# A window-attention and Fourier-mixing kernel on one core: the first ten cycles of its row pipeline get an order of their own

## The chip, the cores and the metric

The kernel runs on one core of one Trainium2 chip. A core has a matrix engine (TensorE, PE in the profile), a vector engine (VectorE, DVE), a scalar engine (ScalarE, ACT), a general engine (GpSimd, POOL) and SyncE (SP), from which nearly all transfers are issued here. Each runs its own list of instructions in program order and waits for others by semaphores. The metric is the time of the kernel on the device in microseconds (us), lower is better. All data is fp32.

## The reference, cut to what matters

The input is 32 images of 56 by 56 tokens with 128 channels. Two layers follow one another:

```python
# layer 0: shifted-window attention (7x7 windows, 4 heads), on the group-normalised image
x = x + window_attention(group_norm(x))
# layer 1: Fourier mixing along both axes (DCT, 32 modes, mix of channels, inverse DCT)
# and then a feed-forward 128 -> 512 -> 128
x = x + feed_forward(fourier(group_norm(x)))
```

The attention of one window of 49 tokens is

```python
q, k, v = win @ w_qkv.T                      # 4 heads of 32 channels
attn = softmax(q @ k.T / sqrt(32) + rel_bias + shift_mask)
out = (attn @ v) @ w_proj.T + b_proj
```

Layer 1 of an image can only begin when the statistics of the whole result of layer 0 of that image are known.

## The kernel before

An image is worked on in 8 rows of 8 windows each. The unit of the program is a *cycle*: in cycle c the attention of row c is begun, and rows c-1, c-2 and c-3 are taken further. Layer 1 of an image starts ten cycles after its first row (`CONV_BEGIN = NWR + 2 = 10`), and from then on its large matmuls lie between those of the attention. In cycles 0 to 9 there is no layer-1 work at all, and the attention of image 0 (and, from cycle 8 on, of image 1) is alone.

The order on PE, ACT, DVE and POOL is the order of the program text (`manual_schedule`). The parts that the change reorders, with the line numbers by which the profile names them:

```python
def attn_qk(im, i):
    q, src = q_sb, im.xw[i][:, :RT]
    pq = attn_bank()
    nc.tensor.matmul(pq[:, :RT], lhsT=im.w[:, 0:C], rhs=src, start=True, stop=True)       # L323 PE
    nc.scalar.activation(q[:, :RT], pq[:, :RT], AF.Identity,
                         bias=im.bias[:, 0:1], scale=QS)                                  # L324 ACT
    pk = attn_bank()
    nc.tensor.matmul(pk[:, :RT], lhsT=im.w[:, C : 2 * C], rhs=src, start=True, stop=True) # L328 PE
    pk3 = pk[:, :RT].rearrange("p (w j) -> p w j", j=WT)
    nc.scalar.activation(k_sb[:, 0], pk3, AF.Identity,
                         bias=im.bias[:, 3:4], scale=heads[:, 0:1])                       # L330 ACT
    nc.vector.tensor_scalar(k_sb[:, 1], pk3, heads[:, 1:2], im.bias[:, 4:5],
                            ALU.mult, ALU.add)                                            # L333 DVE

# attn_v:         16 matmuls (L345), copy of v by ACT (L352)
# attn_scores:    32 matmuls into two banks (L367), bias and mask added by DVE, two tiles (L375)
# attn_max:       row maximum by DVE (L385), subtraction by POOL (L386)
# attn_exp:       exp by ACT (L392)
# attn_divide:    sum and reciprocal by DVE (L397, L399), product by POOL (L400)
# attn_transpose: two times 4 transposes on PE (L411), copied by DVE (L421) and ACT (L419)
# attn_values:    64 matmuls into two banks (L436), copied to oT by ACT (L469) and DVE (L467, three pieces)
# attn_project:   6 or 8 matmuls (L478), added to the image by DVE (L486), row written to memory (L492)
# attn_sums:      square by ACT (L501), two sums for the next statistics by DVE (L503)
# image_group:    4 transposes on PE (L259), copy by ACT (L269), statistics by DVE (L270), addition by POOL (L274)
# image_norm:     statistics of the next image, a chain of small operations between yields:
#                 DVE (L281) / PE (L284), DVE (L286, L288, L290) / PE (L295), DVE, POOL (L299), DVE (L301)
#                 / ACT (L306), PE (L309), DVE (L313 to L315)
```

All of these take their PSUM banks from one set of four, in turn, so each bank has to be emptied before the fourth one after it can be written:

```python
def attn_bank():
    return bank("pa", 4)
```

In cycles 0 to 9 the loop ran these steps, in this order (the calls for layer 1 do nothing there):

```python
# full_first
attn_transpose(c-2); attn_qk(c); next(norm); attn_sums(c-3); attn_divide(c-1)
# half_columns, quarters, eighths
attn_v(c); attn_scores(c); attn_values(c-2)
attn_max(c)
# full_last
next(norm); image groups of the next image; attn_exp(c); attn_project(c-2); next(norm)
```

The load of the second image is called for in cycle 2. Its groups are in cycle 4 (0, 1), cycle 5 (2, 3, 4) and cycle 6 (5, 6, 7), and its normalisation is stepped through in cycle 7.

Of the kernel before, what the change touches and what calls it, by code (L numbers as in the profile page):

```python
# [12 lines left out]
ALU = mybir.AluOpType  # L13
# [35 lines left out]
def swin_fourier_kernel(  # L49
# [266 lines left out]
        yield  # L316


    def attn_qk(im, i):

        q, src = q_sb, im.xw[i][:, :RT]
        pq = attn_bank()
        nc.tensor.matmul(pq[:, :RT], lhsT=im.w[:, 0:C], rhs=src, start=True, stop=True)  # L323
        nc.scalar.activation(  # L324
            q[:, :RT], pq[:, :RT], AF.Identity, bias=im.bias[:, 0:1], scale=QS
        )
        pk = attn_bank()
        nc.tensor.matmul(pk[:, :RT], lhsT=im.w[:, C : 2 * C], rhs=src, start=True, stop=True)  # L328
        pk3 = pk[:, :RT].rearrange("p (w j) -> p w j", j=WT)
        nc.scalar.activation(  # L330
            k_sb[:, 0], pk3, AF.Identity, bias=im.bias[:, 3:4], scale=heads[:, 0:1]
        )
        nc.vector.tensor_scalar(  # L333
            k_sb[:, 1], pk3, heads[:, 1:2], im.bias[:, 4:5], ALU.mult, ALU.add
        )

    def attn_v(im, i, r):

# [43 lines left out]
    def attn_max(r):  # L382
        a3 = a_sb[r % 3].rearrange("p t w j -> p (t w) j")[:, :, 0:WT]
        mx = small.tile([P, 2 * NWR], F32, tag="mx", name="mx")
        nc.vector.tensor_reduce(mx, a3, axis=AX.X, op=ALU.max)  # L385
        nc.gpsimd.tensor_tensor(  # L386
            a3, a3, mx.unsqueeze(2).to_broadcast([P, 2 * NWR, WT]), ALU.subtract
        )
# [82 lines left out]
    def attn_project(im, i):  # L471

        oT = im.oT
        n0, n1 = WS * i // 2, WS * (i + 1) // 2
        base = i // 2 * WS
        pp = attn_bank()
        for n in range(n0, n1):
            nc.tensor.matmul(  # L478
                pp[:TC, (n - n0) * C : (n - n0 + 1) * C],
                lhsT=oT[:, (n - base) * TC : (n - base + 1) * TC],  # L480
                rhs=wproj,
                start=True,
                stop=True,
            )
        piece = im.x[:, n0:n1]
        nc.vector.tensor_tensor(  # L486
            piece,
            pp[:TC, : (n1 - n0) * C].rearrange("p (n c) -> p n c", c=C),
            piece,
            ALU.add,  # L490
        )
        nc.sync.dma_start(  # L492
            im.scr[2 * n0 : 2 * n1].rearrange("(n r) w c -> (r w) n c", r=2), piece
        )
# [204 lines left out]
    def ff_out(im, g):  # L699
        t0, n = sum(FF_GROUPS[:g]), FF_GROUPS[g]  # L700
        k, last = n // P, n % P
        res = im.res
        out_tok = out[im.b].rearrange("h w c -> (h w) c")
        chunks = [P] * k + ([last] if last else [])
        pf = conv_bank()
        for c, m in enumerate(chunks):
            for f in range(NF):
                nc.tensor.matmul(  # L708
                    pf[:m, c * C : (c + 1) * C],
                    lhsT=im.hid[f][:, c * P : c * P + m],  # L710
                    rhs=wff2[:, f],
                    start=(f == 0),
                    stop=(f == NF - 1),
                )
        for c0, c1, m in ((0, k, P), (k, k + 1, last)):
            if m:
                nc.vector.tensor_tensor(  # L717
                    res[:m, c0:c1],
                    pf[:m, c0 * C : c1 * C].rearrange("p (n c) -> p n c", c=C),
                    res[:m, c0:c1],  # L720
                    ALU.add,
                )

        c = 0
        while c < len(chunks):
            m = chunks[c]
            o = t0 + c * P + SS * S
            if o < NT < o + m:
                nc.sync.dma_start(out_tok[o:NT], res[: NT - o, c])
                nc.sync.dma_start(out_tok[: o + m - NT], res[NT - o : m, c])  # L730
                c += 1
                continue
            e = c + 1
            while e < len(chunks) and chunks[e] == m and (o >= NT or o + (e + 1 - c) * m <= NT):
                e += 1
            o %= NT
            nc.sync.dma_start(
                out_tok[o : o + (e - c) * m].rearrange("(n p) c -> p n c", p=m), res[:m, c:e]
            )
            c = e  # L740
# [9 lines left out]
    def row(r):  # L750
        return (images[r // NWR], r % NWR) if 0 <= r < NB * NWR else (None, 0)
# [12 lines left out]
    def full_first(cycle, norm):  # L764
        im, i = row(cycle - 2)
        if im:
            attn_transpose(im, i, cycle - 2)
        im, i = row(cycle)
        if im:
            attn_qk(im, i)  # L770
        for im, c in fourier(cycle):
            for width, g in back_groups(c):
                load_modes(im, width, g)
        next(norm)
        im, i = row(cycle - 3)
        if im:
            attn_sums(im, i)
        for im, c in fourier(cycle):
            if c == 0:
                im.stats = fourier_stats(im)  # L780
                im.cols = {}
                next(im.stats)
                load_columns(im, 0)
                load_columns(im, 1)
        for im, c in fourier(cycle):
            if c in FF_AT:
                ff_in(im, FF_AT.index(c))
        for im, c in fourier(cycle):
            if c == 0:
                next(im.stats)  # L790
        if row(cycle - 1)[0]:
            attn_divide(cycle - 1)

    def half_columns(cycle):
        im, i = row(cycle)
        if im:
            attn_v(im, i, cycle)
        for im, c in fourier(cycle):
            if c == 0:
                for g in range(4):  # L800
                    transform(im, True, g)
            elif c in (1, 2):
                for g in (2 * c - 2, 2 * c - 1):
                    transform(im, False, g)
                    if c == 1:
                        load_columns(im, g + 2)
            elif c == 3:
                for g in range(4):
                    mix(im, False, g)
            elif c in (4, 5):  # L810
                for g in (2 * c - 8, 2 * c - 7):
                    mix(im, True, g)

    def quarters(cycle):
        im, i = row(cycle)
        if im:
            attn_scores(im, i, cycle)
        for im, c in fourier(cycle):
            for width, g in back_groups(c):
                modes_back(im, width, g)  # L820

    def eighths(cycle):
        im, i = row(cycle - 2)
        if im:
            attn_values(im, i, cycle - 2)

    def full_last(cycle, norm):
        next(norm)
        for im, c in fourier(cycle):
            if c in FF_AT:  # L830
                ff_out(im, FF_AT.index(c))
        b, i = divmod(cycle, NWR)
        if b + 1 < NB:
            if i == 2:
                images[b + 1] = image_begin(b + 1)
            for j in {4: (0, 1), 5: (2, 3, 4), 6: (5, 6, 7)}.get(i, ()):
                image_group(images[b + 1], j)
        if row(cycle)[0]:
            attn_exp(cycle)
        im, j = row(cycle - 2)  # L840
        if im:
            attn_project(im, j)
        next(norm)

    def nothing():
# [4 lines left out]
    with tc.manual_schedule(engines={ET.PE, ET.Activation, ET.DVE, ET.Pool}):  # L850
        images[0] = image_begin(0)
        for i in range(NWR):
            image_group(images[0], i)
        for _ in image_norm(images[0]):
            pass
        norm = nothing()
        for cycle in range(NB * NWR + CONV_BEGIN + FF_AT[-1] - NWR + 1):
            full_first(cycle, norm)
            if cycle >= CONV_BEGIN and (cycle - CONV_BEGIN) % NWR != 3:
                quarters(cycle)  # L860
                if row(cycle)[0]:
                    attn_max(cycle)
                half_columns(cycle)
                eighths(cycle)
            else:
                half_columns(cycle)
                quarters(cycle)
                eighths(cycle)
                if row(cycle)[0]:
                    attn_max(cycle)  # L870
            full_last(cycle, norm)
            b, i = divmod(cycle, NWR)
            norm = nothing()
            if i == NWR - 2 and b + 1 < NB:
                norm = image_norm(images[b + 1])
                next(norm)
# [62 lines left out]
```

## Time and profile before

| | before |
|---|---|
| time, median of 3 | 3755.23 us (3753.02 to 3755.56) |
| span of the profiled execution | 3748.9 us |
| PE busy | 3658.2 us, 98% |
| DVE / ACT / POOL busy | 2197.3 / 2131.1 / 1370.9 us |
| mean granted clock of TensorE | 0.993 |

The cycles, by the starts of their query matmuls (L323) in the timeline of PE:

| cycle | 0 | 1 | 2 | 3 | 4 | 5 | 6 | 7 | 8 | 9 | 10 |
|---|---|---|---|---|---|---|---|---|---|---|---|
| start, us | 20.07 | 29.39 | 40.39 | 48.95 | 59.97 | 68.45 | 78.08 | 87.63 | 102.03 | 112.05 | 122.02 |
| length, us | 9.32 | 11.00 | 8.56 | 11.02 | 8.48 | 9.63 | 9.55 | 14.40 | 10.02 | 9.97 | 18.52 |

How to read it: a busy share of 98% for PE says that it nearly always had something in its pipeline, not that it ran at its peak. The granted clock is the share of full speed that the throttle of TensorE allowed. A line of a group or a timeline gives the line of the program, the engine, the operation and its tiles; an idle time in brackets stands before the instruction, with what ended it. The releaser of a wait is inferred from semaphores, and where a wait was for several, the last one is named.

### The profile page before, as it was taken

Reading aid. Unit: us, or ns where it says so; the run is one execution under the profiler, and the core shown is the slowest. Engines: PE = TensorE matmul, PEld = TensorE weight load, DVE = VectorE, ACT = ScalarE, POOL = GpSimd, SP = SyncE. Lnnn points to the kernel's source line nnn. Section 1 sums busy time; section 2 is a strip of 40 time slices with the busy share of each in tenths; the row PEclk is TensorE's granted clock in tenths of the full one; section 3 lists DMA queues with packets and bytes.
Section 4 is the critical chain, followed back from the end, with each engine's and each line's share of the span. In section 5 each row is a group of like instructions: output and inputs, shape, how many; then the busy total and the mean of one; then the engine's idle time right before and its main releaser. Section 6 shows DMA issues by size and latency. Waiting matters only on the chain.

```text
span 3748.9 us, 140497 instructions
## 1 busy us (share of the span) xinstructions
PE 3658.2 (98%) x61632; PEld 2985.1 (80%) x61632; DVE 2197.3 (59%) x4619; ACT 2131.1 (57%) x3809; POOL 1370.9 (37%) x1421
## 2 busy tenths in 40 slices
PE   6799999999999999999999999999999999999998
PEld 5678888888888788888878888888887888888776
DVE  6665665556655556655556655666556566655641
ACT  3455556555565556555555565555655555655553
POOL 4333343333434333343334333333343333333321
PEclk8899999999999999999999999999999999999999
DMA  4233334334333434343343343343333333433332
GB/s 111 78 100 106 107 91 116 105 103 114 91 111 105 110 99 112 96 110 106 104 111 100 98 115 104 100 114 94 110 105 107 103 112 92 115 106 104 94 104 89
DMA packets 687779, 388.95 MB, mean 104 GB/s; under 512 B 40479, under 2 KB 658112, under 8 KB 686912
## 3 DMA queue, kind: packets, MB, share of 16 engines
q1 hardware_dynamic: 686557, 379.65, 36.7%
q8 instruction: 485, 7.95, 0.9%
q14 instruction: 126, 1.03, 0.1%
q10 hardware_dynamic: 611, 0.32, 0.0%
HBM read 218.29 MB, written 161.48 MB: 101 GB/s over the span
## 4 chain that ended last, share of the span: by engine, by line
PE 88%; DVE 7%; ACT 2%; DMA 1%; issue 1%; POOL 0%; SPq 0%; ACTq 0%; POOLq 0%; DVEq 0%
PE pc L708 20%; PE pc L688 15%; PE pa L345 7%; PE pc L572 6%; PE pc L606 5%; PE pa L367 5%; PE pa L411 5%; PE pa L478 5%; PE pc L645 5%; PE pa L436 4%; PE pa L323 4%; PE pa L328 4%; PE pa L259 2%; DVE part L503 1%; DVE st L270 1%; DVE a L375 1%
## 5 line engine op out<-in xcount | busy, mean ns | idle before, releaser
L400 POOL TENSOR_TENSOR a<-a,rs 128x784 f32<-128x784 f32 x256 | 389.5, 1521 | 1366.7 <-DVE rs L399 1254.4
L708 PE MATMUL pc<-wff,hid 128*128 128x128 f32 (+1 forms) x6400 | 778.2, 279 | 0.9 <-ACT hid L696 0.7
L708 PEld LDWEIGHTS pc<-wff,hid 128*128 128x128 f32 (+1 forms) x6400 | 731.0, 189 | 21.0 <-issue 1.9
L688 PE MATMUL pc<-xf,wff 128*128 128x512 f32 (+2 forms) x1792 | 712.8, 540 | 0.0
L696 ACT ACTIVATE hid<-pc,b1sb 128x512 f32<-128x512 f32 (+2 forms) x896 | 540.9, 634 | 102.0 <-PE pc L688 98.7
L688 PEld LDWEIGHTS pc<-xf,wff 128*128 128x128 f32 x1792 | 337.1, 190 | 300.4 <-issue 229.5
L386 POOL TENSOR_TENSOR a<-a,mx 128x784 f32<-128x784 f32 x256 | 389.0, 1520 | 389.2 <-DVE mx L385 384.7
L717 DVE TENSOR_TENSOR res<-pc,res 128x512 f32<-128x512 f32 (+2 forms) x256 | 143.5, 571 | 597.1 <-issue 269.8
L333 DVE TENSOR_SCALAR k<-pa,heads,bqkv 128x392 f32<-128x392 f32 x256 | 175.4, 685 | 420.0 <-ACT k L330 419.9
L419 ACT COPY aT<-pa 113x452 f32<-113x452 f32 x256 | 137.3, 536 | 475.4 <-PE pa L411 475.3
L274 POOL TENSOR_TENSOR xl<-xl,bproj 112x384 f32<-112x384 f32 (+1 forms) x256 | 291.4, 1139 | 227.3 <-PE pa L259 224.2
L392 ACT ACTIVATE a<-a 128x784 f32<-128x784 f32 x256 | 222.6, 869 | 203.5 <-POOL a L386 202.3
L375 DVE TENSOR_TENSOR a<-pa,bm 128x392 f32<-128x392 f32 x512 | 259.5, 549 | 132.1 <-PE pa L367 132.1
L352 ACT COPY v<-pa 128x512 f32<-128x512 f32 x256 | 152.4, 595 | 295.6 <-PE pa L345 295.6
L467 DVE TENSOR_SCALAR oT<-pa,bqkv 128x98 f32<-128x98 f32 (+2 forms) x768 | 171.1, 279 | 248.0 <-PE pa L436 248.0
L678 POOL TENSOR_TENSOR res<-res,b2sb 128x512 f32<-128x512 f32 (+2 forms) x256 | 263.8, 1036 | 101.0 <-DMA res<-scr 101.0
L367 PEld LDWEIGHTS pa<-k,q 64*64 64x64 f32 x8192 | 184.0, 133 | 142.7 <-issue 52.9
L345 PE MATMUL pa<-wn,xw 128*64 128x128 f32 x4096 | 282.1, 280 | 1.1 <-ACT aT L419 1.1
L345 PEld LDWEIGHTS pa<-wn,xw 128*64 128x64 f32 x4096 | 220.0, 137 | 55.3 <-issue 21.9
L478 PE MATMUL pa<-wproj,oT 128*112 128x128 f32 x1792 | 239.3, 274 | 14.3 <-DVE oT L467 11.3
L411 PE MATMUL pa<-ident,a 113*113 113x113 f32 x2048 | 250.0, 265 | 1.5 <-POOL a L400 1.5
L367 PE MATMUL pa<-k,q 64*64 64x98 f32 x8192 | 233.4, 250 | 18.5 <-DVE k L333 18.5
(87 smaller groups left out, 5939.7 us busy)
## 6 DMA issues: line engine op xcount, KB each, us to landing
zscr<-z SPq DMA_DIRECT2D x512, 112.0 KB
htok<-scr SPq DMA_DIRECT2D x256, 196.0 KB
zT<-zscr SPq DMA_DIRECT2D x192, 256.0 KB
res<-scr SPq DMA_DIRECT2D x160, 256.0 KB
out_dram<-res SPq DMA_DIRECT2D x128, 256.0 KB
scr<-xl SPq DMA_DIRECT2D x128, 224.0 KB
xl<-in_x_dram SPq DMA_DIRECT2D x32, 784.0 KB
xl<-in_x_dram SPq DMA_DIRECT2D x32, 672.0 KB
```

The costliest lines, as they stand in the source:

```text
L274: nc.gpsimd.tensor_tensor(piece, piece, bproj.unsqueeze(1).to_broadcast([TC, n1 - n0, C]), ALU.add)
L345: nc.tensor.matmul(pv[hs, j * C : (j + 1) * C], lhsT=im.xw[i][:, w * WT : w * WT + JP], rhs=im.w[:, 2 * C : 3 * C], start=True, stop=True,)
L367: nc.tensor.matmul(ps[hp][HALVES[e], pr * 2 * WT : (pr + 1) * 2 * WT], lhsT=q[cs, w * WT : w * WT + JP], rhs=k_sb[cs, :, w], start=True, s ...
L375: nc.vector.tensor_tensor(a[:, 2 * hp : 2 * hp + 2, :, 0:WT].rearrange("p u w j -> p w u j"), ps[hp][:, :RT].rearrange("p (w u j) -> p w u ...
L386: nc.gpsimd.tensor_tensor(a3, a3, mx.unsqueeze(2).to_broadcast([P, 2 * NWR, WT]), ALU.subtract)
L400: nc.gpsimd.tensor_tensor(a3, a3, rs.unsqueeze(2).to_broadcast([P, 2 * NWR, WT]), ALU.mult)
L411: nc.tensor.transpose(pt[:PW, h * P : h * P + PW], a[:PW, h, 2 * hf : 2 * hf + 2].rearrange("p w j -> p (w j)")[:, :PW], ident[:PW, :PW],)
L478: nc.tensor.matmul(pp[:TC, (n - n0) * C : (n - n0 + 1) * C], lhsT=oT[:, (n - base) * TC : (n - base + 1) * TC], rhs=wproj, start=True, sto ...
L678: nc.gpsimd.tensor_tensor(res[:m, c0:c1], res[:m, c0:c1], b2sb[:m].unsqueeze(1).to_broadcast([m, c1 - c0, C]), ALU.add,)
L688: nc.tensor.matmul(ph[:, :n], lhsT=wff1[:, f * P : (f + 1) * P], rhs=xff[:, t0 : t0 + n], start=True, stop=True,)
L696: nc.scalar.activation(hf[:, :n], ph[:, :n], AF.Relu, bias=b1sb[:, f : f + 1])
L708: nc.tensor.matmul(pf[:m, c * C : (c + 1) * C], lhsT=im.hid[f][:, c * P : c * P + m], rhs=wff2[:, f], start=(f == 0), stop=(f == NF - 1),)
```

## The change

In cycles 0 to 9 the steps are put in an order of their own (`first_rows`). On PE, matmuls that need another engine's answer are to have a group that needs nothing between them and those they depend on: after q and k come the projection of row c-3 and the transposes of row c-2, then the scores; the values of row c-2 come after the scores, and v last. For that the projection moves from the end of cycle c-1 into cycle c, and the exp of row c-1 from the end of its own cycle to behind the keys of row c. In these cycles, too, the second key tile is made by ACT instead of DVE. From cycle 10 on the program is as before. The part that starts the next image is put into a function of its own.

```diff
-    def attn_qk(im, i):
+    def attn_qk(im, i, first):
...
-        nc.vector.tensor_scalar(
-            k_sb[:, 1], pk3, heads[:, 1:2], im.bias[:, 4:5], ALU.mult, ALU.add
-        )
+        if first:
+            nc.scalar.activation(
+                k_sb[:, 1], pk3, AF.Identity, bias=im.bias[:, 4:5], scale=heads[:, 1:2]
+            )
+        else:
+            nc.vector.tensor_scalar(
+                k_sb[:, 1], pk3, heads[:, 1:2], im.bias[:, 4:5], ALU.mult, ALU.add
+            )
...
+    def first_rows(cycle, norm):
+        im, i = row(cycle)
+        if im:
+            attn_qk(im, i, True)
+        if cycle:
+            attn_exp(cycle - 1)
+        next(norm)
+        last, j = row(cycle - 3)
+        if last:
+            attn_project(last, j)
+        im2, i2 = row(cycle - 2)
+        if im2:
+            attn_transpose(im2, i2, cycle - 2)
+        if cycle:
+            attn_divide(cycle - 1)
+        if im:
+            attn_scores(im, i, cycle)
+            attn_max(cycle)
+        if im2:
+            attn_values(im2, i2, cycle - 2)
+        if last:
+            attn_sums(last, j)
+        if im:
+            attn_v(im, i, cycle)
+        next(norm)
+        next_image(cycle)
+        if cycle == CONV_BEGIN - 1:
             attn_exp(cycle)
+            attn_project(im2, i2)
         next(norm)
...
         for cycle in range(NB * NWR + CONV_BEGIN + FF_AT[-1] - NWR + 1):
+            if cycle < CONV_BEGIN:
+                first_rows(cycle, norm)
             else:
+                full_first(cycle, norm)
...
```

## The prediction

> **What bounds the kernel now.** I read the page first, for the shares of the engines and the slices.
>
> ```profile
> PE 3658.2 (98%) x61632; PEld 2985.1 (80%) x61632; DVE 2197.3 (59%) x4619; ACT 2131.1 (57%) x3809; POOL 1370.9 (37%) x1421
> ...
> PE   6799999999999999999999999999999999999998
> ```
>
> TensorE (PE) bounds the whole: nine tenths or more in 37 of 40 slices, and 88% of the chain that ended last. Only the first two slices, some 190 us, have holes; the page's row of granted clock is at 8 tenths there too, and at 9 or more behind. The diff replaces the code of cycles 0 to 9, which is exactly that part, so nothing after about 122 us is touched. Next I put the cycle borders (each cycle's first query matmul, L323, from the timeline of PE) into busy time by stretch. The columns are stretch, length, then busy time (and count) of PE, PEld, DVE, ACT and POOL, granted clock, DMA share, GB/s.
>
> ```profile
> 59.97:68.45 8.48, 6.81 (x141) 5.25 (x139) 6.17 (x14) 4.16 (x9) 2.07 (x2) 0.99 0.21 60
> 87.63:102.03 14.40, 9.22 (x144) 7.20 (x143) 9.29 (x26) 5.16 (x9) 7.88 (x10) 0.85 0.11 31
> 112.05:122.02 9.97, 7.44 (x134) 5.25 (x133) 6.05 (x14) 3.79 (x7) 3.12 (x3) 0.84 0.06 17
> 122.02:140.54 18.52, 13.76 (x248) 11.56 (x247) 8.17 (x20) 7.60 (x13) 4.11 (x5) 0.74 0.33 80
> ```
>
> No engine is full in these cycles, so it is a chain of waits. Cycle 9 shows it, first on PE (start, length, what; in brackets the idle time and its releaser), then on VectorE (DVE).
>
> ```profile
> 112.05 1.54 PE L323 MATMUL pa<-xw,wn 128*128 128x392 f32 x2
> 113.39 1.50 PE L328 MATMUL pa<-xw,wn 128*128 128x392 f32 x2
> 114.81 1.09 PE L345 MATMUL pa<-wn,xw 128*64 128x128 f32 x16
> 116.44 0.90 PE L367 MATMUL pa<-k,q 64*64 64x98 f32 x32 [0.53 <-DVE k L333]
> 117.27 0.81 PE L436 MATMUL pa<-aT,v 49*32 49x49 f32 x64
> 120.08 1.10 PE L478 MATMUL pa<-wproj,oT 128*112 128x128 f32 x8 [2.00 <-DVE oT L467]
> 121.01 1.21 PE L411 MATMUL pa<-ident,a 113*113 113x113 f32 x8
> ```
> ```profile
> 115.69 0.69 DVE L333 TENSOR_SCALAR k<-pa,heads,bqkv 128x392 f32<-128x392 f32 x1 [3.48 <-ACT k L330]
> 116.30 0.54 DVE L503 TENSOR_REDUCE part<-xl 112x32 f32<-112x384 f32 x1
> ...
> 118.38 0.97 DVE L375 TENSOR_TENSOR a<-pa,bm 128x392 f32<-128x392 f32 x2
> 119.27 0.66 DVE L467 TENSOR_SCALAR oT<-pa,bqkv 128x98 f32<-128x98 f32 x3
> ```
>
> Two holes: the scores wait for the second key tile, and the projection waits about 2 us for oT. DVE idles 3.48 us until the keys come and then has everything at once: key tile, sums, softmax sum, scores, oT. And q and k took 1.54 and 1.50 us here, against 0.84 and 0.82 us at 48.95 and 49.62: each hole is followed by some microseconds at half clock.
>
> **What the Trainium skill says.** TensorE: Matmul & The Clock Gate, "What's actually happening": the array runs at half rate after an idle window of about 3.4 us and at full rate after a busy one. The trace agrees in kind: granted 0.50 at 58 to 60 us after the 2.00 us hole, 1.00 two slices on. ScalarE: Activation LUTs, "What ACT_TABLE_LOAD costs": an activation is about 186 ns + 0.833 ns an element, 93 ns more for each per-partition operand; with 392 elements and two operands 699 ns (estimate from the page). The first key tile, which has this form, takes 677 ns. SBUF — State Buffer, "Who interferes with whom": a DVE instruction with two SBUF inputs and a GpSimd (POOL) instruction that reads SBUF lock each other out. The trace agrees: the same 128x1 subtraction takes 0.97 us inside a POOL addition, ending with it, and 0.37 us near the end of another.
>
> ```profile
> 14.41 1.27 POOL L274 TENSOR_TENSOR xl<-xl,bproj 112x512 f32<-112x512 f32 x1
> ...
> 14.74 0.97 DVE L288 TENSOR_TENSOR d<-mv,gm 128x1 f32<-128x1 f32 x1
> ...
> 91.62 0.37 DVE L288 TENSOR_TENSOR d<-mv,gm 128x1 f32<-128x1 f32 x1
> ```
>
> **The change, part by part.** No matmul is added or removed. One DVE instruction of 0.69 us a cycle becomes one of ScalarE (ACT) of 0.68 us. The rest is order. On PE the new cycle c is q(c), k(c), projection(c-3), transposes(c-2), scores(c), values(c-2), v(c), image groups. From start-to-start distances at full clock (cycles 4 to 6 and 11): q 0.67, k 0.75, projection 0.74 or 0.89, transposes 0.79, scores 0.83, values 0.78, v 0.92: **5.6 us of PE work**. DVE after the change has, by start distances, projection add 0.55, aT 0.55, sm 0.99, rs 0.17, scores 0.95, mx 0.87, oT 0.58, two sums 1.05: 5.7 us.
>
> *A regular cycle.* The loop I find longest: q and k on PE (1.42), ACT first key tile (start +0.05), second 0.58 later, exp 0.58 later, lasting 0.87; DVE sm to its end 0.99, rs 0.25, first scores tile out of its PSUM bank 0.55; the v matmuls, which take that bank by the rotation of four, 0.92; then the next q. Sum 6.21, with some 0.15 for handoffs **6.35 us**. Beside it lie projection and transposes (1.6 us while ACT makes the keys, about 1.5 us, so this hole is filled), values (they wait until about 4.1 for ACT's aT, behind exp) and POOL (3.04 us of 6.35). PE is 88% busy, so I take the full clock.
>
> *The special cycles.*
> - Start: q(0) stays at 20.07. The bias table on DVE ends at 27.1; before, the key tile queued behind it and the first scores tile left at 29.49. By ACT the keys are ready near 24.4, scores are done at 26, and DVE adds at 27.14: 2.35 us earlier. In cycle 2 the chain is max subtraction of row 1 (to 37.2), exp 38.1, aT 38.6, values 39.4, v 41. I put **q(3) at 42** (before: 48.95).
> - Cycle 3: 6.6. Cycles 4, 5, 6 carry 2, 3 and 3 image groups of 0.37 us on PE, and the third waits for oT's bank: 7.05, 7.65, 7.65.
> - Cycle 7 carries the next image's normalisation. Its two small DVE operations now stand early, while POOL still works at the image additions: up to 2.5 us, I take 1.5 more, so v ends at 7.9. Then ve waits for the sums on DVE (9.7), POOL's rstd (0.55) for the max subtraction, then nb, and six matmuls, cold, 1.3: **12.0** (before 14.40).
> - Cycle 8: 6.35 and 1.5 for a cold start: 7.9. Cycle 9 ends in its own exp and projection(7), which needs oT at about 7.2: 7.25 + 0.9 + transposes 0.8 = 8.95 to q(10) (before 9.97).
>
> Sum: 42 + 6.6 + 7.05 + 7.65 + 7.65 + 12.0 + 7.9 + 8.95 = **99.8 us for q(10)**, against 122.02: 22.2 us. In cycle 10 q and k should be at full clock, 1.4 less on the path to the statistics. I take 1 off for what I can't see: **22.6 us, 0.6%**; 3755.2 - 22.6 = 3732.6. After cycle 11 PE is full and its program is unchanged, so the shift should stay.
>
> **Rivals.**
> 1. *The next image is not there.* Its load is issued from 46.73 to 54.3 us, behind the constants on SyncE's queue, not by the cycle. The new cycle 4 wants the first half at about 55 us instead of 65.86. DMA moved 238 to 260 GB/s at 50 to 56 and was quiet from 58, so the wait would be 0 to 4 us; saving 19 to 22.
> 2. *ACT or DVE takes the place of the old waits.* Both queues are in order: exp stands ahead of aT, and sm, rs and the scores are in front of mx and oT. If hand-offs cost twice my figure, or the clock still drops, a cycle is 7.3 to 8 and the saving 12 to 16. For it: DVE's 5.7 us of 6.35. Against it: DVE's queue ends before the next projection add needs it.
> 3. *The gain is given back.* Cycle 10 needs the columns by DMA after the last projection, and the statistics chain leaves PE idle 3.88 us there. Against it: that chain starts from the projection, so it moves along; weights had landed by about 58 us. If it held, 5 to 10 us remain.
> 4. *More is saved*: cold stretches vanish wholly and cycle 7 is 10.5: 26 to 28 us.
>
> **Range and chances.** The code touched lasts 102 us of 3755 (20.07 to 122.02). PE's own work in it is some 53 us (3.2 in cycles 0 and 1, 4.8 in cycle 2, 5.6 in each later one, 3 of image groups), so at most 50 us can go and 2% (75 us) is out of reach; a loss of 2% would need these cycles to take 74% longer. Runs before lie within 2.6 us. 27 to 28 us saved gives the low end 3726; a mix of rivals 1 and 2, 12 us, gives 3743.
>
> **What would show it.** L323 starts of cycles 3 and 10 near 42 and 100; regular cycles near 6.4 us with clock 1.00; no wait of the projection for oT; scores released by ACT, not DVE, within 0.2 us; v waiting for the scores tile on DVE; cycle 7 still the longest, with nb before its hole. The prediction is wrong if a DMA wait stands before the image transposes of cycle 4, if regular cycles are over 7.3 us, or if the stretch from q(10) to q(11) grows beyond 18.5 us.

## The result and the profile after

| | before | changed |
|---|---|---|
| time, median | 3755.39 us (4 runs, 3753.02 to 3755.84) | 3732.79 us (4 runs, 3730.88 to 3733.75) |
| span of the profiled execution | 3748.9 us | 3729.1 us |
| start of cycle 10 (L323) | 122.02 us | 103.62 us |
| start of cycle 11 | 140.54 us | 120.75 us |

The ratio is 0.994 (95% interval 0.9923 to 0.9958): some 22 us, 0.6%. A later comparison, five runs of the changed kernel beside nine of before, gave 3730.03 against 3751.05 us, 0.9945 (0.9933 to 0.9958). In the two traces the lead is 18.4 us at the start of cycle 10, 19.8 at the start of cycle 11, and 19.8 at the end: all of it is made in the part that was changed, and nothing is given back. That the last two figures agree so well is chance, though. The stretch from the start of cycle 11 to the end has the same program in every kernel of this document; it took 3608.36 and 3608.35 us in these two traces, but between 3604.7 and 3614.0 us in all thirteen. What a part of the change is worth is therefore better read in the first cycles than at the end. (The profiled execution of before is a short one, 3750.7 us, which is why the traces show 3 us less than the medians.)

The page of the changed kernel: engines, then the slices of PE.

```profile
PE 3647.9 (98%) x61632; PEld 2980.9 (80%) x61632; DVE 2191.3 (59%) x4609; ACT 2139.8 (57%) x3819; POOL 1371.6 (37%) x1421
...
PE   6899999999999999999999999999999999999998
```

PE's first two slices have gone from 6 and 7 tenths to 6 and 8; its row of granted clock shows 9 tenths or more throughout, where the first two slices were at 8 (in a second trace of the changed kernel the first slice is at 8). Busy time by cycle, from the same borders as before (cycles 3, 4 and 9; columns as in the prediction):

```profile
40.34:46.82 6.48, 5.90 (x132) 4.63 (x130) 4.76 (x11) 4.45 (x8) 3.04 (x3) 1.00 1.02 432
46.82:56.91 10.09, 6.83 (x142) 5.68 (x141) 7.92 (x18) 5.34 (x10) 5.04 (x6) 1.00 1.01 255
...
94.36:103.62 9.26, 7.67 (x148) 6.39 (x147) 8.43 (x19) 5.76 (x10) 4.73 (x4) 1.00 0.08 21
```

A regular cycle (cycle 3) takes 6.48 us at full clock, with PE busy for 5.90 of it. Cycle 4 is out of line: 10.09 us, with the DMA share at 1.01. Cycle 9 on PE, to be laid beside the one of before:

```profile
94.36 0.93 PE L323 MATMUL pa<-xw,wn 128*128 128x392 f32 x2
95.12 0.82 PE L328 MATMUL pa<-xw,wn 128*128 128x392 f32 x2
...
97.32 0.91 PE L372 MATMUL pa<-k,q 64*64 64x98 f32 x32
...
99.75 1.09 PE L350 MATMUL pa<-wn,xw 128*64 128x128 f32 x16 [0.50 <-DVE a L380]
101.90 1.10 PE L483 MATMUL pa<-wproj,oT 128*112 128x128 f32 x8 [1.05 <-DVE oT L472]
```

The query matmuls took 1.54 us here before and take 0.93 now. There is no hole before the scores (L372): projection and transposes lie ahead of them while ACT makes the keys. v waits 0.50 us for a scores tile to leave its bank, and only the second projection of this last cycle still waits for oT (1.05 us). And the end of cycle 4:

```profile
52.22 1.09 PE L350 MATMUL pa<-wn,xw 128*64 128x128 f32 x16 [0.50 <-DVE a L380]
56.07 1.00 PE L259 MATMUL pa<-ident_x,xl 112*128 112x112 f32 x8 [2.76 <-DMA xl<-in_x_dram]
...
57.72 1.51 PE L328 MATMUL pa<-xw,wn 128*128 128x392 f32 x2
```

After v PE waits 2.76 us for a transfer, the load of the second image, and then runs its key matmuls at 1.51 us instead of 0.82. This is the one wait in the new part that no engine can shorten by computing faster. SyncE's queue shows why the image is late (the last of the constants, then the five pieces of the image):

```profile
39.04 8.13 SPq L125 DMA_DIRECT2D b2sb<-in_b_dram  x1
47.21 8.75 SPq L114 DMA_DIRECT2D xl<-in_x_dram  x5
```

The image is not issued before 47.21 us, behind all constants, whatever the cycle is in which the program calls for it.

### The profile page after: what moved, and what is told of

Same layout as the page of the kernel before. It is cut to its first block, busy times and chain, and to the rows that moved or that the text cites. A ratio compares the mean times of both kernels' runs of the same rounds, so it can differ in the third digit from the quotient of the medians.

```text
span 3729.1 us, 140497 instructions
## 1 busy us (share of the span) xinstructions
PE 3647.9 (98%) x61632; PEld 2980.9 (80%) x61632; DVE 2191.3 (59%) x4609; ACT 2139.8 (57%) x3819; POOL 1371.6 (37%) x1421
## 4 chain that ended last, share of the span: by engine, by line
PE 89%; DVE 6%; ACT 2%; DMA 1%; SPq 1%; issue 1%; POOL 0%; ACTq 0%; DVEq 0%; POOLq 0%
PE pc L713 20%; PE pc L693 15%; PE pa L350 7%; PE pc L611 6%; PE pc L577 6%; PE pa L372 5%; PE pa L416 5%; PE pa L483 5%; PE pc L650 5%; PE pa L441 4%; PE pa L323 4%; PE pa L328 4%; PE pa L259 2%; DVE part L508 1%; DVE st L270 1%; DVE a L380 1%
## 5 line engine op out<-in xcount | busy, mean ns | idle before, releaser
L372 PEld LDWEIGHTS pa<-k,q 64*64 64x64 f32 x8192 | 183.5, 132 | 135.3 <-issue 53.9
L390 DVE TENSOR_REDUCE mx<-a 128x16 f32<-128x784 f32 x256 | 247.1, 965 | 5.7
L402 DVE TENSOR_REDUCE sm<-a 128x16 f32<-128x784 f32 x256 | 245.6, 959 | 4.7 <-ACT a L397 4.7
```

The costliest lines, as they stand in the source:

```text
L372: nc.tensor.matmul(ps[hp][HALVES[e], pr * 2 * WT : (pr + 1) * 2 * WT], lhsT=q[cs, w * WT : w * WT + JP], rhs=k_sb[cs, :, w], start=True, s ...
```

## The experiments

To compare across traces, I use the time from the start of cycle 0 to the start of cycle 10, both at L323 (some programs have other line numbers), because the start itself moves by up to 1 us from run to run: 101.95 us before, 83.50 in the changed kernel, 84.50 in its second trace. Device times of one kernel scatter by several us (25 runs of before lie between 3748.69 and 3762.77); the medians of before, run beside each group of experiments, are 3753.57 us (order, key tile, fillers, early image), 3753.61 (early image with key tile, exp twice, normalisation) and 3751.05 (projection, v, the changed kernel again). Theory A was that the gain is the order, with exp behind the keys and the projection between keys and scores as the parts that carry it; the rivals are given with each.

### The order without the key tile on ScalarE

```diff
-            attn_qk(im, i, True)
+            attn_qk(im, i, False)
```

> The new order, but with the second key tile by DVE as before. Theory A (the order is the change, the engine of the key tile matters at the start only): the first cycle begins its scores after DVE's bias table, about 2.3 us later than with ACT, and a regular cycle grows by 0.1 to 0.3 us (6.5 to 6.7), so some 16 of the 20 us saved by the trace remain, time about 3737. Theory B (taking 0.69 us a cycle off DVE is what lets the new order work, as DVE has 5.7 us of 6.4): a regular cycle is 7.0 or more, and no more than 12 us remain, time 3743 or more.

Measured: 3732.74 us, 0.9943 (0.993 to 0.9955). From cycle 0 to cycle 10 it is 82.44 us, 1.06 less than in the changed kernel. So the key tile on ScalarE brought nothing that can be seen. The trace says why. Scores of cycle 0, image transposes of cycle 4, and the keys behind them:

```profile
28.20 1.58 PE L372 MATMUL pa<-k,q 64*64 64x98 f32 x32 [4.85 <-DVE k L338]
...
56.74 1.01 PE L259 MATMUL pa<-ident_x,xl 112*128 112x112 f32 x8
...
58.26 0.82 PE L328 MATMUL pa<-xw,wn 128*128 128x392 f32 x2
```

The scores of cycle 0 do come late, 28.20 us against 24.52, after a wait of 4.85 us for DVE, and cycle 3 is 6.68 us instead of 6.48. But the program then reaches the image's transposes at 56.74, when the image is there: it waits nothing, PE doesn't cool, and the keys run in 0.82 us. The changed kernel was there at 53.3 and had to wait until 56.07. Theory A's cycle length held and its total didn't, because it left out the image. Theory B (7.0 us a cycle) falls.

### The key tile on ScalarE in the old order

```diff
-            attn_qk(im, i)
+            attn_qk(im, i, cycle < CONV_BEGIN)
```

> The old order, with the second key tile of cycles 0 to 9 by ACT. Theory A: the scores of cycle 0 come 2 to 3 us earlier, the later cycles gain 0.1 to 0.2 us each because the key tile on DVE waited for ACT's first one anyway: 3 to 5 us in all, time about 3751. Theory B: the sums, the softmax sum and oT on DVE come 0.6 us earlier in every cycle, so 8 us or more, time 3747 or less.

Measured: 3748.59 us, 0.9988 (0.9982 to 0.9995), 5.0 less than before; 98.71 us from cycle 0 to 10, 3.2 less. The total is what theory A said, but it does not come about in the same way. Cycle 0 is 4.2 us shorter, and cycles 1 and 2 lose 2.5 us of that again. In ScalarE's queue the key tiles stand behind exp, which waits for GpSimd's subtraction, so the scores of cycle 1 wait for the keys:

```profile
33.38 1.58 PE L372 MATMUL pa<-k,q 64*64 64x98 f32 x32 [4.55 <-ACT k L334]
```

At the start of cycle 3 a lead of 1.7 us is left; cycle 3 adds 1.3, and cycles 4 to 9 add 0.2 together. The hole before the projection is the same as it was, 2.04 us in cycle 9, released by oT.

### Filling the holes without taking the waits away

```diff
+    def filler(cycle, n):
+        im, i = row(cycle)
+        if im and cycle < CONV_BEGIN:
+            for _ in range(n):
+                pf = conv_bank()
+                nc.tensor.matmul(pf[:, :RT], lhsT=im.w[:, 0:C],
+                                 rhs=im.xw[i][:, :RT], start=True, stop=True)
...
     def quarters(cycle):
+        filler(cycle, 1)
...
+        filler(cycle, 2)
         im, j = row(cycle - 2)
         if im:
             attn_project(im, j)
```

The repeated query matmuls go to a bank that nothing reads and that layer 1 does not yet use; outputs and waits are as before.

> The old order, with query matmuls repeated into a PSUM bank that nothing reads: one before the scores and two before the projection in cycles 0 to 9, to fill the holes without taking the waits away. If part of the loss before was the clock that falls behind each hole: the query, key, projection and transpose matmuls of cycles 3, 7, 8 and 9 run at full speed, the tenth cycle begins 5 to 8 us earlier than before although PE has 20 us more work, time about 3749. If only the waits count: no gain, or 1 to 5 us lost where a filler lasts longer than the hole.

Measured: 3749.9 us, 0.999 (0.9983 to 0.9996), 3.7 less than before; 98.79 us from cycle 0 to 10, 3.2 less, although PE has more work. Query and scores of cycle 9:

```profile
109.85 0.84 PE L323 MATMUL pa<-xw,wn 128*128 128x392 f32 x2
...
113.91 0.91 PE L367 MATMUL pa<-k,q 64*64 64x98 f32 x32 [0.69 <-DVE k L333]
```

The queries take 0.84 us (before: 1.54) and the keys 0.82 (before: 1.50); the projection's wait is down to 0.48 us. Cycle 3 falls from 11.02 to 9.20 us and cycle 7 from 14.40 to 12.10. But cycle 9 falls by 0.54 us only, although query and key matmuls take 1.42 us from the first's start to v, 1.34 less than before: the scores still wait for the keys. From v to the scores it is 2.64 us now and was 1.63; the filler lies in that stretch, and the wait behind it is 0.69 instead of 0.53 us, so 1.0 of the 1.34 us is spent there. Cycle 8 stays slow, as the hole in the normalisation before it could not be filled. The gain is less than the 5 to 8 us I expected also because cycles 4 to 6 got longer by 0.25 to 1.84 us, where image transposes stood in the hole already. The parts that got shorter (cycles 0 to 2 by 0.77, 3, 7, 8 and 9) sum to 5.6 us. So 3 to 6 of the 18 us come back when holes are filled and the waits are left as they are. This is not the whole share of the clock, as the fillers take time of their own and cycle 8 stayed slow; how the rest divides between clock and waits these runs don't show.

### The image loaded early

```diff
+    xls[1] = load_image(1)
     w1sb = const_load([P, NM, C], w1, "w1sb")
```

> The changed kernel, with the load of the second image issued before the two large mixing weights (2 MB each) instead of behind all constants. If the image is what cycle 4 waited for (2.76 us, and 1.5 us of slow clock behind it): no DMA wait before the image transposes, cycle 4 at 7.1 and cycle 5 at 7.7 us, 3.5 to 4.2 us saved, time about 3729. If another wait takes its place, or the weights are then late: under 1 us.

Measured: 3729.96 us, 0.9936 (0.9923 to 0.9948); from cycle 0 to 10 79.82 us, 3.7 less than in the changed kernel. The interval doesn't set it apart from the changed kernel's 0.994; the first cycles of the trace do. Image transposes and the keys behind them:

```profile
53.63 1.02 PE L260 MATMUL pa<-ident_x,xl 112*128 112x112 f32 x8
...
55.16 0.82 PE L329 MATMUL pa<-xw,wn 128*128 128x392 f32 x2
```

No wait and full clock: cycle 4 is 7.29 us instead of 10.09, cycle 5 is 7.66 instead of 8.81. The mixing weights, which now come after the image, are not waited for in cycles 10 to 14. At the start of cycle 11 the lead over the changed kernel is 4.0 us (116.73 against 120.75), but the two profiled executions end within 0.3 us of each other, as the same program behind cycle 11 took 3612.1 us here and 3608.4 there. So that the image was what cycle 4 waited for is shown; that the kernel as a whole gains 4 us by it is not.

### Both: early image, key tile by VectorE

The early load, and `attn_qk(im, i, False)`.

> The early image load, and the second key tile by DVE. Theory A (the engine of the key tile is worth 3 to 4 us, 2.3 at the start and 0.2 a cycle, and in the changed kernel the wait for the image hid that): cycle 10 begins 3 to 4.5 us later than with the early image and the key tile by ACT, time about 3733. Theory B (the engine makes no difference): within 1 us of it, time about 3730.

Measured: 3733.66 us, 0.9948 (0.9936 to 0.9961); 85.03 us from cycle 0 to 10, 5.2 more than with the key tile by ScalarE. So that tile is worth something once the image is there in time. 3.66 of it are made before cycle 3 (24.12 against 20.46 us from the start of cycle 0), the rest is 0.2 to 0.4 us in each of cycles 3 to 6 and 9. The order alone had the same program in cycles 0 to 2 and took 22.80 us for them, so 1.3 us of this can be chance: 4 to 5 us is what the runs support. The changed kernel hides it behind the load.

### exp at the end of its own cycle

```diff
-        if cycle:
-            attn_exp(cycle - 1)
         next(norm)
...
-        if cycle == CONV_BEGIN - 1:
+        if im:
             attn_exp(cycle)
+        if cycle == CONV_BEGIN - 1:
             attn_project(im2, i2)
```

> The changed kernel, but exp of row c at the end of its own cycle, where it was before; the rest of the new order stays. Theory A (the loop before was max, subtraction, exp, and behind exp in ACT's queue the next query and key tiles; moving exp behind the keys is the main part): a regular cycle is about 8.5 us instead of 6.4, cycle 10 begins 12 us or more later than in the changed kernel, time about 3744. Theory B (the filled holes of PE are the main part): a cycle of 7.0 or less, time 3738 or less.

Measured: 3734.73 us, 0.995 (0.9938 to 0.9962); 84.03 us, 0.5 more than in the changed kernel and 4.2 more than with the early image. Neither number of the theories was right: cycle 3 is 7.26 us, between 8.5 and 7.0. In that cycle, all engines, ACT's queue and the scores:

```profile
46.50 0.87 ACT L397 ACTIVATE a<-a 128x784 f32<-128x784 f32 x1 [1.38 <-POOL a L391]
...
48.30 0.68 ACT L334 ACTIVATE k<-pa,bqkv,heads 128x392 f32<-128x392 f32 x1
...
49.03 0.91 PE L372 MATMUL pa<-k,q 64*64 64x98 f32 x32 [0.49 <-ACT k L334]
```

exp waits for POOL's subtraction, and query and both key tiles stand behind it, so the scores wait again. The ring of exp, the three tiles on ScalarE, scores, maximum and subtraction is 7.26 us long; I had put it at 8.5 by adding exp to the end of a cycle that otherwise kept the timing of the changed one. The regular cycle loses 0.8 us by it, but 7.26 us a cycle brings the program to the image's transposes at 59.00 us, when the image is there, and the total hardly shows it. In cycle 6, which has three image groups on PE, the place of exp makes no difference: 7.55 us here, 7.61 in the changed kernel.

### Only exp moved, in the old order

```diff
             attn_qk(im, i)
+        if 0 < cycle < CONV_BEGIN:
+            attn_exp(cycle - 1)
...
-        if row(cycle)[0]:
+        if row(cycle)[0] and cycle >= CONV_BEGIN - 1:
             attn_exp(cycle)
```

> The old order, with only the exp of row c-1 moved behind the keys of row c in cycles 1 to 9. Theory A: cycles of 8.3 us or so where they were 8.5 to 11, no slow clock in them, 6 to 9 us saved of the 20, time about 3746. Theory B (without the groups between, exp's place changes nothing as the projection still waits for oT): 2 us or less, time 3752 or more.

Measured: 3747.24 us, 0.9983 (0.9977 to 0.999), 6.4 less than before; 97.37 us from cycle 0 to 10, 4.6 less. The time is in theory A's range, but not by its mechanism. The gain lies in cycles 0 to 2 (4.0 us), 3 (1.7) and 7 (1.1); cycles 8 and 9 are within 0.1 us of before, and cycles 4 to 6 are 0.7 to 0.9 us longer. I had expected no slow clock. Slices of 2 us in cycles 4 and 5:

```profile
60.00:62.00 2.00, 0.96 (x11) 0.81 (x8) 1.97 (x8) 0.71 (x2) 1.25 (x1) 1.00 0.23 70
62.00:64.00 2.00, 1.99 (x17) 1.75 (x16) 2.00 (x5) 0.72 (x3) 1.15 (x2) 1.00 0.20 61
...
68.00:70.00 2.00, 1.09 (x66) 0.96 (x47) 1.97 (x5) 0.45 (x1) 0.83 (x1) 0.94 0.40 119
70.00:72.00 2.00, 2.00 (x12) 2.00 (x11) 2.00 (x6) 1.10 (x3) 0.82 (x2) 0.50 0.00 0
```

The clock drops to 0.50 at 70 us, behind a hole of only 0.91 us before the image transposes, and again at 80 us behind one of 1.04. In both cases PE had been busy for about half of the slice before (1.09 and 0.96 us). But the slice from 60 to 62 us has the same hole (1.04 us) and the same busy time (0.96 us), and the clock stays at 1.00 behind it. The projection waits as long as ever, 2.05 us in cycle 9 (at 115.72).

### The projection at the end of its own cycle

```diff
-        if last:
-            attn_project(last, j)
...
         if cycle == CONV_BEGIN - 1:
             attn_exp(cycle)
+        if im2:
             attn_project(im2, i2)
```

> The changed kernel, with the projection of row c-2 at the end of its own cycle again, behind v; the rest of the new order stays. Theory A (the projection between keys and scores, one cycle later, takes away the wait for oT that was about 2 us): it waits again, 0.8 to 1 us after v, and no longer fills the time in which ACT makes the keys; a regular cycle is 7.8 to 8.1 us instead of 6.5, time about 3739 to 3741. Theory B (only the place of exp and of v counts): 6.7 or less a cycle, time 3733 or less.

Measured: 3731.46 us, 0.995 (0.9937 to 0.9962), beside 3730.03 for the changed kernel on the same chip; 85.78 us from cycle 0 to 10 against 84.50. The projection at the end of cycle 3 and the next scores:

```profile
51.22 1.10 PE L483 MATMUL pa<-wproj,oT 128*112 128x128 f32 x8 [1.05 <-DVE oT L472]
...
54.98 0.90 PE L372 MATMUL pa<-k,q 64*64 64x98 f32 x32 [0.54 <-ACT k L334]
```

The cycle itself is as theory A had it, and a little worse: 8.37 us instead of 6.48 (7.14 on its own chip, where it began with queries of 1.58 us), with 1.05 us of waiting for oT and 0.54 us for the keys. Its total was wrong again. Cycle 4 takes 8.15 us and meets the image at 58.48 without a wait (9.53 us in the changed kernel on the same chip), and in cycle 7 the projection lies in the hole of the normalisation, so that cycle 7 takes 10.74 instead of 12.46 us.

### The normalisation step moved, and v moved

On top of the early image, the second step of the normalisation (`next(norm)`) goes from behind v to before `attn_divide` in `first_rows`:

```diff
             attn_transpose(im2, i2, cycle - 2)
+        next(norm)
         if cycle:
             attn_divide(cycle - 1)
...
             attn_v(im, i, cycle)
-        next(norm)
         next_image(cycle)
```

> The kernel with the early image load, and with the second step of the next image's normalisation moved in cycle 7 from behind the v matmuls to before the softmax sum, so that the variance, its power and the shift are ready before the hole. If the 2.55 us hole before the six bias matmuls and the slow clock behind it are what cycle 7 and 8 cost beyond a regular one: the hole goes, cycle 7 falls from 12.3 to about 10, cycle 8 from 8.7 to about 6.7, some 4 us less than with the early image alone, time about 3726. If the wait only moves (VectorE now waits for GpSimd's power before the softmax sum): 1 us or less.

Measured: 3726.31 us, 0.9931 (0.9918 to 0.9945); 75.17 us from cycle 0 to 10, 4.65 less than with the early image alone. The six bias matmuls, first in the changed kernel, then here with the queries of cycle 8 behind them:

```profile
84.52 1.22 PE L309 MATMUL pa<-nb,wqkv 128*128 128x1 f32 x6 [2.55 <-DVE nb L301]
```
```profile
78.84 0.83 PE L310 MATMUL pa<-nb,wqkv 128*128 128x1 f32 x6
80.11 0.93 PE L324 MATMUL pa<-xw,wn 128*128 128x392 f32 x2 [0.44 <-ACT wn L307]
```

The hole of 2.55 us is gone, and the queries of cycle 8 run at 0.93 instead of 1.66 us. Cycle 7 takes 10.43 us instead of 12.28, cycle 8 6.46 instead of 8.75 (12.47 and 8.59 with the early image alone). The time is the expected one, 27.3 us less than before where the early image alone gave 23.6, but the intervals overlap; what is shown is the gain in cycles 7 and 8.

On top of that, v between transposes and scores:

```diff
         if im:
+            attn_v(im, i, cycle)
             attn_scores(im, i, cycle)
...
             attn_sums(last, j)
-        if im:
-            attn_v(im, i, cycle)
```

> The kernel with early image and early normalisation step, and with the v matmuls between the transposes and the scores instead of last. In the changed kernel v waits 0.5 us in each cycle for a scores tile to leave its bank. Theory A (the loop through exp, softmax sum, scores tile and v sets 6.45 us): v drops out of the loop, a regular cycle is 5.9 to 6.1 us, cycle 10 begins 2.5 to 4 us earlier, time about 3723. Theory B (what sets it is VectorE or the first key tiles): within 0.1 us a cycle, time 3726; or the scores come later and a cycle is 6.7.

Measured: 3721.75 us, 0.9923 (0.991 to 0.9937); but 74.94 us from cycle 0 to 10, only 0.23 less. Regular cycles are 6.69 and 6.38 us (cycles 3 and 8), as before the move (6.49 and 6.46); cycles 5 and 6 are 0.3 to 0.5 shorter. Cycles 0 to 8 together are 1.8 us shorter, and cycle 9 loses 1.55 of that again (10.82 us): its second projection waits 2.14 us for oT instead of 1.05. Theory A falls: v does not wait for the scores tile any more, and the regular cycle keeps its length, because the scores come later and so does oT. Both projections of cycle 9:

```profile
86.86 0.88 PE L484 MATMUL pa<-wproj,oT 128*112 128x128 f32 x6 [0.55 <-DVE oT L473]
...
93.27 1.10 PE L484 MATMUL pa<-wproj,oT 128*112 128x128 f32 x8 [2.14 <-DVE oT L473]
```

The 0.50 us wait of v was not what set the cycle alone; several loops of nearly the same length lie behind one another. The lower time of this version is not explained by its first ten cycles (from cycle 0 to cycle 11 it takes 1.2 us more than the one before it), and its interval overlaps theirs. Against the changed kernel in the same comparison it is 8.3 us faster, and the ranges (3719.21 to 3724.17 and 3727.02 to 3732.76) don't meet. It has the lowest time of those that ran, but is not told apart from the version without the move of v: 29.3 us less than before of its own comparison, beside 27.3.

The changed kernel in that comparison:

> The changed kernel once more, on the same chip as the other two, to compare with: 0.9935 to 0.9955 of before, some 20 us less; cycle 4 waits 1 to 3 us for the second image.

It gave 0.9945, with cycle 4 at 9.53 us. The v matmuls of its cycle 2, and its image transposes:

```profile
39.94 1.97 PE L350 MATMUL pa<-wn,xw 128*64 128x128 f32 x16 [0.50 <-DVE a L380]
...
56.98 1.73 PE L259 MATMUL pa<-ident_x,xl 112*128 112x112 f32 x8 [1.51 <-DVE part L508]
```

The wait of 1.51 us is put down to a sum of VectorE. With the early image, though, the transposes begin before that sum (53.63 against 54.52 us), so they don't depend on it. The last piece of the image was issued at 55.85 us here; I take this wait, too, for the image's, but this trace alone does not show it.

No run tried the new places of the transposes, the values or the sums alone, and none has the early image with exp or the projection in its old place.

## Why the prediction was right, and where it was not

The time was predicted at 3732.6 and measured at 3732.79 us. By its steps it was less exact than that.

| step | predicted, us | trace, us | second trace, us |
|---|---|---|---|
| start of cycle 3 | 42 | 40.34 | 41.84 |
| cycle 3 | 6.6 | 6.48 | 7.14 |
| cycle 4 | 7.05 | 10.09 | 9.53 |
| cycle 5 | 7.65 | 8.81 | 8.54 |
| cycle 6 | 7.65 | 7.61 | 7.61 |
| cycle 7 | 12.0 | 12.28 | 12.46 |
| cycle 8 | 7.9 | 8.75 | 8.27 |
| cycle 9 | 8.95 | 9.26 | 9.26 |
| start of cycle 10 | 99.8 | 103.62 | 104.65 |
| cycle 10 | 1.4 less than 18.52 | 17.13 | 15.74 |

- **The bound.** That these cycles are a chain of waits, and that the shift stays because PE is full behind them, held within the scatter of that long stretch: 19.8 us at cycle 11 and 19.8 at the end of the traces, 22.6 by the medians.
- **The regular cycle.** 6.35 predicted, 6.48 measured, at clock 1.00 (7.14 in the second trace, where it began with queries of 1.58 us), no wait of the projection for oT, v waiting 0.50 us for the scores tile. The loop I added up is of the right length, but not the only one of that length: with v taken out of it (the last experiment) the cycle stayed at 6.4 to 6.7.
- **Cycles 4 and 5, the step that failed.** The sum left the second image out; it stood among the rivals with "0 to 4 us". It came true: 2.76 us of waiting, and slow matmuls behind it, so that the two cycles took 4.2 us more than their sum in the prediction. A DMA wait before the image transposes of cycle 4 was also the first of the prediction's own signs of being wrong, and in this step it was wrong. With the image loaded early, the two cycles take 7.29 and 7.66 us, and the start of cycle 11 is 116.73 us, beside 99.8 and 17.1, 116.9 by the prediction's steps. So the steps described a kernel without that wait, with smaller errors that cancel (cycle 3 starts 1.3 us earlier than predicted there, cycles 7 and 8 take 1.2 us more).
- **Why the total fitted all the same.** Cycle 10 began 3.8 us later than predicted, and I had taken 1 us off for what I could not see; on the other side, the medians differ by 22.6 us where the traces differ by 19.8. The agreement within 0.2 us is luck; agreement within 3 or 4 is what the steps deserve.
- **The key tile and the start.** The scores of cycle 0 came 3.4 us earlier (24.52 against 27.88) and the first tile left its bank 2.31 us earlier (27.18), as worked out, but this did not reach the end: order alone took as long. Where the image is early, the key tile is worth 4 to 5 us.
- **Cycle 7.** Predicted for the right reasons (variance, POOL's power, shift, six bias matmuls behind the sums and the maximum subtraction); the trace has the same chain, ending in nb and a hole of 2.55 us.
- **Rival 2** (other queues take the place of the old waits) did not come true: 6.5 us (7.1 in the second trace), not 7.3 to 8. **Rival 3** (given back) did not: 17.13 us in cycle 10. **Rival 4** (more is saved) needs the early load and the earlier normalisation step (27.3 us by the medians).
- **The range.** 27 to 28 us less than 3755.2 would have put its low end at 3727 to 3728, not at 3726.

What part carries the gain? Two of its parts alone bring 3.2 us (key tile) and 4.6 us (exp) from cycle 0 to 10, the holes filled with useless work 3.2, and the whole 18.5; and each part taken away from the whole costs 2 or less (key tile none, exp 0.5, projection 1.3 on its own chip). In large part this is because what is lost before cycle 4 would have been spent waiting for the image; for the key tile the runs with the early image show it, for exp and the projection it is argued. A single cycle at full clock, which has no such floor, shows the parts better, and it repeats well: with all of them, cycle 3 took 6.48, 6.48 and 6.49 us (changed kernel, early image, early normalisation step; the 7.14 of the second trace began at half clock). It takes 6.68 without the key tile, 7.26 without exp's move and 8.37 without the projection's. Cycle 6, with its three image groups, took 7.60 or 7.61 with all of them, and 8.00, 7.55 and 8.25 in the same order. By both, the projection's place counts most; exp's counts in cycle 3 and not in cycle 6.

## What to carry to other kernels

When a chain before the steady part is made shorter, look for the transfer that was hidden behind its old length: here it was ready at 56 us and wanted at 53, and it then hid the worth of the key tile, so that taking this part away seemed to cost nothing. Judge the parts by the length of single cycles that ran at full clock, not by the total, and by more than one cycle. In a queue that is served in order, the place of an operation that waits for a third engine (exp here) matters as much as the engine on which it runs.

## What the runs showed of the hardware that was not expected

The clock of PE does not follow from the length of a hole alone. With exp moved alone it fell to 0.50 behind holes of 0.91 and 1.04 us, shorter than the idle window of about 3.4 us in the prediction, and stayed at 1.00 behind another hole of 1.04 us in the same trace, with the same 0.96 us of busy time in the 2 us around it. In the changed kernel it stayed at 1.00 through cycle 2, with holes of 1.56 and 1.14 us; in the second trace of the same program it fell to 0.50 at 40 us, behind a hole of 0.93 and one of 0.50 us. So the v matmuls of cycle 2 took 1.09 us in one execution and 1.97 in the other. The length of a stretch that is not quite full can thus change by about 1 us from one execution to the next, for no reason in the program.
